# A GRU, attention and AUGRU recommender on one core: attention MLP as three matmuls on shared rows, blockwise softmax, two lagged halves

## The chip, the cores and the metric

The kernel runs on one core of a Trainium2 chip. The core has a matmul engine (TensorE, PE in the profile), a vector engine (VectorE, DVE), an engine for activation functions (ScalarE, ACT), a general one (GpSimd, POOL) and SyncE (SP), which here issues every DMA. Each engine works through its own queue in order; semaphores tie them together. SBUF holds tiles of 128 partitions, matmul results land in PSUM (8 banks, each 128 x 512 in f32), everything larger lies in DRAM. The metric is the device time of one execution in microseconds.

## The reference

A batch of B = 1024 users, T = 100 steps, all widths 128, all in f32. What is computed:

```python
hist_sum = (item_hist * mask[:, :, None]).sum(1) / length[:, None]
# GRU over the 100 steps, all states kept
r = sigmoid(x @ Wir + h @ Whr + b);  z = sigmoid(x @ Wiz + h @ Whz + b)
n = tanh(x @ Win + bin + r * (h @ Whn + bhn))
h = (1 - z) * n + z * h                       # keys[t] = h
# attention: MLP of 512 -> 80 -> 40 -> 1, ReLU after each layer
feat  = concat([keys, q, keys - q, q * keys]) # q: the item's embedding
score = where(mask == 1, mlp(feat), -inf)
pooled = einsum('bt,btd->bd', softmax(score, axis=1), keys)
att = pooled.T[:T]                            # row t weighs step t of the AUGRU
# AUGRU over keys
r = sigmoid([h, k] @ Wr + br);  u = att[t] * sigmoid([h, k] @ Wu + bu)
h = (1 - u) * h + u * tanh([h * r, k] @ Wh + bh)
# state at each user's length, then an MLP of 640 -> 200 -> 80 -> 1 with sigmoids
out = mlp(concat([user, item, hist_sum, item * hist_sum, h_last]))
```

The AUGRU needs the pooled keys, these need the softmax over all 100 scores of a user, and a score needs the GRU's state of its step. Users don't depend on each other.

## The kernel before

Features lie on the partitions and the batch on the free dimension. A PSUM bank holds 512 columns, so the batch is worked in two halves (`HB = 512`, `NH = 2`). One f32 product, `nc.tensor.matmul` of a 128 x 128 weight with 128 x 512 data, appears in the profile as two MATMUL instructions, each with its weight load (PEld). The code is a tile program: it states operations on named tiles, and a scheduler sorts them at compile time into one fixed order for each engine, by their place in the program and by when it reckons them ready, and adds the semaphores. An operation that stands late in the program can so come early in its queue. A pool with `bufs=n` gives n buffers in turn to tiles of one tag; a DMA into a buffer waits until its last reader is done.

The work stands in four stages, one after the other.

1. GRU, attention scores and history sum (loop at L172). For each step t it loads x (512 KB, both halves) and the mask row spread over the partitions. For each half, `gru` (L114) makes six products: the gate r from x and h (L118, with `wih` and `whh`), the two halves of n kept apart, and z. ACT makes r (L129) and z (L134), DVE forms the argument of tanh from PSUM (L136, L139), ACT takes tanh (L141), and three DVE operations (L143 to L145) make the new state `hn`. GpSimd multiplies x by the mask and adds it to `hist` (L183, L184). For each half, `score` (L147) makes `kq` = state times item on DVE (L150), two products for layer 0 (L152, L153: 80 result rows), adds the part of the item alone and takes ReLU (L155, L156), one product of 80 rows for layer 1 (L158), ReLU (L160), and one product of 40 rows for layer 2 (L163). That last one uses a sliding window of a zero matrix with one column, so that the score of step t lands on partition t of a PSUM tile that is kept for the whole stage. The state goes to DRAM (L188), but for the last `RES` = 16 steps, which stay in SBUF.
2. Softmax and pooled keys. The scores are transposed so that users are on partitions, masked, exponentiated, transposed back and written to DRAM. For each of 100 steps the weights' row is loaded spread over the partitions (L256), the keys too (L259, 84 steps), DVE multiplies them (L262), and PE adds them up in PSUM with the identity as weight (L264, 200 products). The pooled rows times one over the sum (L250, L277), zero from a user's length on (L278), go to DRAM.
3. AUGRU (loop at L318). For each step the row of weights `at` and the keys are loaded; for each half `augru` (L295) makes three gates of two products each (L297 to L310), with ACT for sigmoid and tanh (L300, L306, L312), GpSimd for u times at (L307) and DVE for the rest (L301, L313 to L315).
4. Prediction MLP (L339 to L372), 13 products for each half.

Of the kernel before, what the change touches and what calls it, by code (L numbers as in the profile page):

```python
# [17 lines left out]
P = 128  # L18
# [4 lines left out]
NG = B // P  # L23
A0, A1 = 80, 40
M0, M1 = 200, 80
MC = 100
RES = 16
# [3 lines left out]
def kernel(ctx: ExitStack, tc: tile.TileContext, a: dict, out: bass.AP):  # L31
    """Features lie on the partitions and the batch on the free dim throughout.

    1: GRU over the steps, with the attention MLP's scores and the masked history sum.
    2: masked softmax over the steps and the pooled keys.
    3: AUGRU over the steps.
    4: the prediction MLP.
    The keys of the last RES steps stay in SBUF; the others go through DRAM.
    """
# [3 lines left out]
    resp = ctx.enter_context(tc.tile_pool(name="resp", bufs=1))  # L43

    keys_d = dram.tile([T - RES, P, B], F32, name="keys_d")
    mask_d = dram.tile([T, B], F32, name="mask_d")
    e_d = dram.tile([T, B], F32, name="e_d")
    att_d = dram.tile([T, B], F32, name="att_d")
    res = resp.tile([P, RES, B], F32, name="res")
# [7 lines left out]
    mask_ti = load("mask_ti", [T, B], dt=I32)  # L57
# [3 lines left out]
    bhh = load("bhh", [P, 3])  # L61
    item = load("item", [P, B])
    w0 = load("w0", [P, 4, A0])
    b0 = load("b0", [A0, 1])
    w1 = load("w1", [A0, A1])
    b1 = load("b1", [A1, 1])
    b2 = load("b2", [T, 1], a["b2"].partition_broadcast(T))
    w2 = const.tile([A1, 2 * T - 1], F32, name="w2")
    nc.vector.memset(w2, 0.0)
    nc.sync.dma_start(out=w2[:, T - 1 : T], in_=a["w2"])  # L70

    mask_tf = const.tile([T, B], F32, name="mask_tf")
# [5 lines left out]
    ones = const.tile([T, P], F32, name="ones")  # L78
    nc.vector.memset(ones, 1.0)
# [7 lines left out]
    wk = const.tile([P, A0], F32, name="wk")  # L87
    nc.vector.tensor_add(wk, w0[:, 0, :], w0[:, 2, :])
    wq = const.tile([P, A0], F32, name="wq")
    nc.vector.tensor_sub(wq, w0[:, 1, :], w0[:, 2, :])  # L90
# [3 lines left out]
    h0 = const.tile([P, B], F32, name="h0")  # L94
    nc.vector.memset(h0, 0.0)
    q0 = const.tile([A0, B], F32, name="q0")
    s_t = const.tile([T, B], F32, name="s_t")

# [1 line left out]
    with tc.tile_pool(name="xp", bufs=3) as xp, tc.tile_pool(  # L100
        name="hp", bufs=3
    ) as hp, tc.tile_pool(name="wp", bufs=2) as wp, tc.tile_pool(
        name="ps_s", bufs=1, space=PSUM
    ) as ps_s, tc.tile_pool(name="ps_g", bufs=4, space=PSUM) as ps_g, tc.tile_pool(
        name="ps_a", bufs=2, space=PSUM
    ) as ps_a:
        for i in range(NH):
            pq = ps_a.tile([A0, HB], F32, tag="a", name="pq")
            nc.tensor.matmul(pq, lhsT=wq, rhs=item[:, ts(i, HB)], start=True, stop=True)
            nc.scalar.activation(q0[:, ts(i, HB)], pq, AF.Identity, bias=b0)  # L110

        sc = [ps_s.tile([T, HB], F32, tag=f"sc{i}", name=f"sc{i}") for i in range(NH)]

        def gru(x, h, hn, cols):  # L114
            def gate(g, parts):
                ps = ps_g.tile([P, HB], F32, tag="g", name=f"ps{g}")
                for n, (w, v) in enumerate(parts):
                    nc.tensor.matmul(  # L118
                        ps,
                        lhsT=w[:, g, :],  # L120
                        rhs=v[:, cols],
                        start=(n == 0),
                        stop=(n == len(parts) - 1),
                    )
                return ps

            pr = gate(0, ((wih, x), (whh, h)))
            r = wp.tile([P, HB], F32, name="r")
            nc.scalar.activation(r, pr, AF.Sigmoid, bias=brz[:, 0:1])  # L129
            ph = gate(2, ((whh, h),))  # L130
            pi = gate(2, ((wih, x),))
            pz = gate(1, ((wih, x), (whh, h)))
# [3 lines left out]
            nc.vector.scalar_tensor_tensor(  # L136
                out=u, in0=ph, scalar=bhh[:, 2:3], in1=r, op0=ALU.add, op1=ALU.mult
            )
# [4 lines left out]
            nc.vector.tensor_sub(d, h[:, cols], n)  # L143
            nc.vector.tensor_mul(d, z, d)  # L144
            nc.vector.tensor_add(hn[:, cols], n, d)  # L145

        def score(t, k, i):  # L147
            cols = ts(i, HB)
            kq = wp.tile([P, HB], F32, name="kq")
            nc.vector.tensor_mul(kq, k[:, cols], item[:, cols])  # L150
            p0 = ps_a.tile([A0, HB], F32, tag="a", name="p0")
            nc.tensor.matmul(p0, lhsT=wk, rhs=k[:, cols], start=True, stop=False)  # L152
            nc.tensor.matmul(p0, lhsT=w0[:, 3, :], rhs=kq, start=False, stop=True)  # L153
            f0 = wp.tile([A0, HB], F32, name="f0")
            nc.vector.tensor_add(f0, p0, q0[:, cols])  # L155
            nc.scalar.activation(f0, f0, AF.Relu)  # L156
            p1 = ps_a.tile([A1, HB], F32, tag="a", name="p1")
            nc.tensor.matmul(p1, lhsT=w1, rhs=f0, start=True, stop=True)  # L158
            f1 = wp.tile([A1, HB], F32, name="f1")
            nc.scalar.activation(f1, p1, AF.Relu, bias=b1)  # L160
            # Only column t of this window of w2 is not zero: the scores of step t
            # come onto partition t.
            nc.tensor.matmul(  # L163
                sc[i],
                lhsT=w2[:, T - 1 - t : 2 * T - 1 - t],
                rhs=f1,
                start=(t == 0),
                stop=(t == T - 1),
            )

        h = h0
        for t in range(T):  # L172
            x = xp.tile([P, B], F32, name="x")
            nc.sync.dma_start(out=x, in_=a["hist_x"][t])
            m = xp.tile([P, B], F32, name="m")
            nc.sync.dma_start(out=m, in_=mask_d[t].partition_broadcast(P))
            if t < T - RES:
                hn = hp.tile([P, B], F32, name="hn")
            else:
                hn = res[:, t - (T - RES), :]  # L180
            for i in range(NH):
                gru(x, h, hn, ts(i, HB))
            nc.gpsimd.tensor_mul(m, x, m)  # L183
            nc.gpsimd.tensor_add(hist, hist, m)  # L184
            for i in range(NH):
                score(t, hn, i)
            if t < T - RES:
                nc.sync.dma_start(out=keys_d[t], in_=hn)  # L188
            h = hn

        for i in range(NH):
            nc.scalar.activation(s_t[:, ts(i, HB)], sc[i], AF.Relu, bias=b2)

# [1 line left out]
    wr = load("wr", [P, 2, P])  # L195
    wu = load("wu", [P, 2, P])
    wh = load("wh", [P, 2, P])
    br = load("br", [P, 1])
    bu = load("bu", [P, 1])
    bh = load("bh", [P, 1])  # L200
    user = load("user", [P, B])
    m0 = load("m0", [P, 5, M0])
    c0 = load("c0", [MC, M0 // MC])
    m1 = load("m1", [MC, M0 // MC, M1])
    c1 = load("c1", [M1, 1])
    m2 = load("m2", [M1, 1])
    c2 = load("c2", [1, 1])
    len_i = load("len_i", [P, B], a["len_i"].partition_broadcast(P), dt=I32)
    length = const.tile([P, B], F32, name="length")
    nc.vector.tensor_copy(length, len_i)  # L210

# [1 line left out]
    with tc.tile_pool(name="sp", bufs=1) as sp, tc.tile_pool(  # L213
        name="kp", bufs=4
    ) as kp, tc.tile_pool(name="ps_t", bufs=2, space=PSUM) as ps_t, tc.tile_pool(
        name="ps_p", bufs=1, space=PSUM
    ) as ps_p:
        mask_i = sp.tile([P, NG, T], I32, name="mask_i")
        nc.sync.dma_start(out=mask_i, in_=a["mask"].rearrange("(g p) t -> p g t", p=P))
        on = sp.tile([P, NG, T], F32, name="on")  # L220
        nc.vector.tensor_scalar(on, mask_i, 1.0, None, ALU.is_equal)

        # Scores are not negative, so 0 in the masked places leaves the maximum right.
        e = sp.tile([P, NG, T], F32, name="e")
        for g in range(0, NG, 4):
            pt = ps_t.tile([P, 4, P], F32, tag="t", name="pt")
            for j in range(4):
                nc.tensor.transpose(pt[:, j, :T], s_t[:, ts(g + j, P)], ident[:T, :T])
            nc.vector.tensor_mul(e[:, g : g + 4, :], pt[:, :, :T], on[:, g : g + 4, :])
        top = sp.tile([P, NG], F32, name="top")  # L230
        nc.vector.tensor_reduce(top, e, AX.X, ALU.max)
        nc.vector.tensor_sub(e, e, top.unsqueeze(2).to_broadcast([P, NG, T]))
        nc.scalar.activation(e, e, AF.Exp)
        nc.vector.tensor_mul(e, e, on)

        e_t = sp.tile([T, B], F32, name="e_t")
# [203 lines left out]
```

## Time and profile before

| what | value |
|---|---|
| time, median of 3 runs | 3267.64 us (3263.62 to 3268.73) |
| span of the profiled execution, first to last instruction | 3262.5 us |
| DMA traffic | 348.46 MB, mean 107 GB/s |
| loads of keys in stages 2 and 3 | 168 of 512 KB, 6.0 us to landing |
| loads of x, of the mask row | 100 each of 512 KB, 3.7 us to landing |
| granted clock of TensorE, mean | 0.990 |

The profile shows one execution. For it only the span is known; the runs' times also hold what lies around it. A row of instruction groups reads: line, engine, operation, output <- inputs, shapes, count, then busy time, mean duration in ns, the idle time of the engine just before them and what ended it. In the chain of waits each piece is the work that the next piece was waiting for. The granted clock is the share of TensorE's full clock that the throttle let through. TensorE's busy time is modelled for pipelined matmuls; their spacing in the chain is the safer price.

### The profile page before, as it was taken

How to read it: one execution, taken by the hardware profiler on the slowest of the kernel's cores; microseconds unless marked ns; L12 is line 12 of the kernel's file. 1: busy time of each engine (PE TensorE's matmuls, PEld its weight loads, DVE VectorE, ACT ScalarE, POOL GpSimd, SP SyncE). 2: the span in 40 equal slices, each digit the busy share in tenths (PEclk: the TensorE clock that was granted, in tenths of full speed). 3: DMA queues.
4: the chain of work that ended last, by engine and by line, in shares of the span. 5: the costliest groups of instructions: out<-in, count | busy, mean ns of one | idle time of the engine just before them, and what ended most of it. 6: DMA issues, size and time to landing. Idle time of an engine off the chain costs nothing.

```text
span 3262.5 us, 22072 instructions
## 1 busy us (share of the span) xinstructions
PE 3128.4 (96%) x6876; PEld 1163.6 (36%) x6876; DVE 1659.5 (51%) x2325; ACT 1093.2 (34%) x1617; POOL 765.2 (23%) x408
## 2 busy tenths in 40 slices
PE   7999999999999999999999977769999999999998
PEld 2333333333333333333333322224444444444443
DVE  5555554554555555555545544435555555555554
ACT  2333333333333333333333310003434343444433
POOL 3223223223222222232232100002222222222221
PEclk9999999999999999999999979999999999999999
DMA  4222222222222222222211049983333333333110
GB/s 158 84 79 89 84 84 84 84 85 87 81 90 84 78 90 84 79 89 84 75 54 58 20 138 378 397 324 103 99 102 99 101 103 103 103 103 103 65 52 13
DMA packets 98464, 348.46 MB, mean 107 GB/s; under 512 B 13109, under 2 KB 13977, under 8 KB 98346
## 3 DMA queue, kind: packets, MB, share of 16 engines
q1 hardware_dynamic: 98346, 347.05, 31.1%
q8 instruction: 54, 0.88, 0.1%
q14 instruction: 64, 0.52, 0.1%
HBM read 301.73 MB, written 45.27 MB: 106 GB/s over the span
## 4 chain that ended last, share of the span: by engine, by line
PE 80%; DVE 8%; DMA 5%; ACT 4%; issue 1%; SPq 0%; ACTq 0%; DVEq 0%; POOLq 0%; POOL 0%
PE ps L118 27%; PE sc L163 6%; PE p L158 6%; PE pr L297 5%; PE pu L303 5%; PE pr L298 5%; PE pu L304 5%; PE ph L310 5%; PE ph L309 5%; DMA k<-keys_d 4%; PE p L152 3%; PE p L153 3%; DVE d L144 2%; ACT z L134 2%; ACT f L156 2%; DVE hn L145 2%
## 5 line engine op out<-in xcount | busy, mean ns | idle before, releaser
L118 PE MATMUL ps<-x,wih 128*128 128x512 f32 x1200 | 617.6, 610 | 1.0 <-DMA x<-in_hist_x 1.0
L183 POOL TENSOR_TENSOR m<-x,m 128x1024 f32<-128x1024 f32 x100 | 275.3, 2753 | 1322.9 <-DMA x<-in_hist_x 1307.1
L307 POOL TENSOR_TENSOR u<-u,at 128x512 f32<-128x512 f32 x200 | 252.7, 1264 | 1131.6 <-ACT u L306 1131.6
L118 PE MATMUL ps<-hn,whh 128*128 128x512 f32 x1008 | 501.0, 592 | 0.0
L313 DVE TENSOR_TENSOR d<-d,hn 128x512 f32<-128x512 f32 x198 | 137.1, 692 | 459.4 <-ACT d L312 459.4
L155 DVE TENSOR_TENSOR f<-p,q 80x512 f32<-80x512 f32 x200 | 136.6, 683 | 434.7 <-PE p L153 434.7
L118 PEld LDWEIGHTS ps<-x,wih 128*128 128x128 f32 x1200 | 211.9, 189 | 358.2 <-issue 307.0
L156 ACT ACTIVATE f<-f 80x512 f32<-80x512 f32 x200 | 126.0, 630 | 536.0 <-DVE f L155 536.0
L118 PEld LDWEIGHTS ps<-hn,whh 128*128 128x128 f32 x1008 | 191.6, 190 | 245.4 <-issue 225.3
L264 PE MATMUL pool<-eb,ident 128*128 128x512 f32 x400 | 197.8, 623 | 63.1 <-DVE eb L262 63.0
L141 ACT ACTIVATE n<-u,bih 128x512 f32<-128x512 f32 x200 | 144.4, 722 | 306.9 <-DVE u L139 306.9
L158 PE MATMUL p<-f,w 80*40 80x512 f32 x400 | 212.2, 612 | 28.0 <-ACT f L156 28.0
L184 POOL TENSOR_TENSOR hist<-hist,m 128x1024 f32<-128x1024 f32 x100 | 235.5, 2355 | 7.8
L163 PE MATMUL sc<-f,w 40*100 40x512 f32 x400 | 221.7, 634 | 0.8 <-ACT f L160 0.8
L144 DVE TENSOR_TENSOR d<-z,d 128x512 f32<-128x512 f32 x200 | 142.4, 712 | 155.8 <-ACT z L134 154.9
L136 DVE SCALAR_TENSOR_TENSOR u<-ps,bhh,r 128x512 f32<-128x512 f32 x200 | 150.2, 751 | 126.6 <-PE ps L118 123.7
L153 PE MATMUL p<-kq,w 128*80 128x512 f32 x400 | 212.5, 613 | 1.7 <-DVE kq L150 1.7
L129 ACT ACTIVATE r<-ps,brz 128x512 f32<-128x512 f32 x200 | 137.2, 686 | 226.2 <-PE ps L118 225.7
L312 ACT ACTIVATE d<-ph,bh 128x512 f32<-128x512 f32 x200 | 137.4, 687 | 206.8 <-PE ph L310 206.8
L306 ACT ACTIVATE u<-pu,bu 128x512 f32<-128x512 f32 x200 | 137.4, 687 | 205.5 <-PE pu L304 205.5
L300 ACT ACTIVATE r<-pr,br 128x512 f32<-128x512 f32 x200 | 137.4, 687 | 204.1 <-PE pr L298 204.1
L310 PE MATMUL ph<-r,wh 128*128 128x512 f32 x400 | 204.3, 592 | 0.0
(113 smaller groups left out, 3546.4 us busy)
## 6 DMA issues: line engine op xcount, KB each, us to landing
k<-keys_d SPq DMA_DIRECT2D x168, 512.0 KB, 6.0
x<-in_hist_x SPq DMA_DIRECT2D x100, 512.0 KB, 3.7
m<-mask_d SPq DMA_DIRECT2D x100, 512.0 KB, 3.7
eb<-e_d SPq DMA_DIRECT2D x100, 512.0 KB, 5.5
at<-att_d SPq DMA_DIRECT2D x100, 512.0 KB, 4.5
keys_d<-hn SPq DMA_DIRECT2D x84, 512.0 KB, 2.6
item<-in_item SPq DMA_DIRECT2D x1, 512.0 KB
user<-in_user SPq DMA_DIRECT2D x1, 512.0 KB, 4.9
```

The costliest lines, as they stand in the source:

```text
L118: nc.tensor.matmul(ps, lhsT=w[:, g, :], rhs=v[:, cols], start=(n == 0), stop=(n == len(parts) - 1),)
L144: nc.vector.tensor_mul(d, z, d)
L153: nc.tensor.matmul(p0, lhsT=w0[:, 3, :], rhs=kq, start=False, stop=True)
L156: nc.scalar.activation(f0, f0, AF.Relu)
L158: nc.tensor.matmul(p1, lhsT=w1, rhs=f0, start=True, stop=True)
L163: nc.tensor.matmul(sc[i], lhsT=w2[:, T - 1 - t : 2 * T - 1 - t], rhs=f1, start=(t == 0), stop=(t == T - 1),)
L183: nc.gpsimd.tensor_mul(m, x, m)
L184: nc.gpsimd.tensor_add(hist, hist, m)
L264: nc.tensor.matmul(pool[i], lhsT=ident, rhs=eb[:, ts(i, HB)], start=(n == 0), stop=(n == T - 1),)
L297: nc.tensor.matmul(pr, lhsT=wr[:, 1, :], rhs=k[:, cols], start=True, stop=False)
L307: nc.gpsimd.tensor_mul(u, u, at[:, cols])
L310: nc.tensor.matmul(ph, lhsT=wh[:, 0, :], rhs=r, start=False, stop=True)
```

## The change

The whole computation is kept; its order and its layout change.

- *Shared rows.* The attention MLP's hidden rows lie side by side on 128 partitions: rows 0 to 39 hold layer 1, rows 40 to 95 and 97 to 120 layer 0, and row 96 the score (`F1`, `F0` and `SC` in the diff). The step's `attend` adds three products into one PSUM tile: `wk` on the state, `wkq` on state times item, `w12` on the tile `mv` of the attend before, which holds layer 0 of step t - 1 and layer 1 of step t - 2 (w12 holds the weights of layers 1 and 2). One DVE addition and one ReLU serve the three layers. A score so comes out two steps late, as row 96 of `mv`, and a DMA copies it to its row of a block tile `s_b`.
- *Blocks.* Scores are collected in three blocks that end at steps 48, 92 and 100 (`ENDS`). When a block is complete, `softmax` transposes it, takes the running maximum, exponentiates, adds to the running sum and writes the weights and the factor for what was pooled so far to DRAM.
- *Pooling on VectorE.* `pool` loads a row of weights and a step's keys (256 KB each) and does a multiplication and an addition into `pooled` in SBUF; one key a step, or two when more are left than steps; all that is left after the last step.
- *Two streams.* Each half is an object of its own. Half 1 runs `LAG` = 5 ticks behind half 0, and a half starts its AUGRU `GAP` = 4 ticks after its last GRU tick. All pools are open for the whole kernel; GRU and AUGRU share six PSUM buffers, attention and softmax have two.
- Loads are for 512 columns; all keys go through DRAM (`RES` is gone); step 0 leaves out the products with the zero state; a half's part of the history features and its prediction MLP are emitted in its own stream.

The diff, cut to its core:

```diff
-RES = 16
+F1 = slice(0, A1)
+F0 = (slice(A1, 96), slice(97, 121))
+W0 = (slice(0, 96 - A1), slice(96 - A1, A0))
+SC = 96
+ENDS = (48, 92, T)
+LAG = 5
+GAP = 4
...
+    for f, s in zip(F0, W0):
+        nc.vector.tensor_add(wk[:, f], w0[:, 0, s], w0[:, 2, s])
+        nc.vector.tensor_copy(wkq[:, f], w0[:, 3, s])
+        nc.vector.tensor_sub(wq[:, f], w0[:, 1, s], w0[:, 2, s])
+        nc.sync.dma_start(out=w12[f, F1], in_=a["w1"][s, :])
...
+    nc.sync.dma_start(out=w12[F1, SC : SC + 1], in_=a["w2"])
...
+    xp = ctx.enter_context(tc.tile_pool(name="xp", bufs=5))
+    hp = ctx.enter_context(tc.tile_pool(name="hp", bufs=8))
+    wp = ctx.enter_context(tc.tile_pool(name="wp", bufs=3))
+    sp = ctx.enter_context(tc.tile_pool(name="sp", bufs=2))
+    kp = ctx.enter_context(tc.tile_pool(name="kp", bufs=4))
+    ps = ctx.enter_context(tc.tile_pool(name="ps", bufs=6, space=PSUM))
+    pa = ctx.enter_context(tc.tile_pool(name="pa", bufs=2, space=PSUM))
...
+        def gru(self, t):
+            cols = self.cols
+            x = xp.tile([P, HB], F32, name="x")
+            nc.sync.dma_start(out=x, in_=a["hist_x"][t][:, cols])
+            m = xp.tile([P, HB], F32, name="m")
+            nc.sync.dma_start(out=m, in_=mask_d[t, cols].partition_broadcast(P))
...
+            nc.gpsimd.tensor_mul(m, x, m)
+            nc.gpsimd.tensor_add(hist[:, cols], hist[:, cols], m)
+            nc.sync.dma_start(out=keys_d[t][:, cols], in_=hn)
+            self.h = hn
...
+        def attend(self, t):
+            parts = []
+            if t < T:
+                kq = wp.tile([P, HB], F32, name="kq")
+                nc.vector.tensor_mul(kq, self.h, item[:, self.cols])
+                parts += [(wk, self.h), (wkq, kq)]
+            if self.mv is not None:
+                parts += [(w12, self.mv)]
+            p = pa.tile([P, HB], F32, tag="a", name="pm")
+            for n, (w, v) in enumerate(parts):
+                nc.tensor.matmul(
+                    p, lhsT=w, rhs=v, start=(n == 0), stop=(n == len(parts) - 1)
+                )
+            f = wp.tile([P, HB], F32, name="f")
+            nc.vector.tensor_add(f, p, q0[:, self.cols])
+            mv = wp.tile([P, HB], F32, name="mv", bufs=4)
+            nc.scalar.activation(mv, f, AF.Relu)
+            self.mv = mv
+            s = t - 2
...
+            nc.sync.dma_start(out=self.s_b[s - a0 : s - a0 + 1, :], in_=mv[SC : SC + 1, :])
+            if s == ENDS[self.block] - 1:
+                self.softmax()
...
+        def softmax(self):
...
+            nc.vector.tensor_mul(e[:, :, :n], pt[:, :, :n], on)
+            top = sp.tile([P, GH], F32, name="top", bufs=5)
+            nc.vector.tensor_reduce(top, e[:, :, :n], AX.X, ALU.max)
+            if j:
+                nc.vector.tensor_max(top, top, self.top)
+                nc.vector.tensor_sub(e[:, :, n], self.top, top)
...
+            nc.scalar.activation(e[:, :, :rows], e[:, :, :rows], AF.Exp)
+            nc.vector.tensor_mul(e[:, :, :n], e[:, :, :n], on)
+            den = sp.tile([P, GH], F32, name="den", bufs=5)
+            nc.vector.tensor_reduce(den, e[:, :, :n], AX.X, ALU.add)
...
+            nc.sync.dma_start(out=e_d[j][:rows, self.cols], in_=e_t[:rows, :])
+            if j:
+                self.todo.append((j, n, None))
+            self.todo += [(j, t - a0, t) for t in range(a0, a1)]
+            if last:
+                self.todo.append((j, n + 1, None))
...
+        def pool(self, count):
+            for _ in range(min(count, len(self.todo))):
+                j, row, t = self.todo.pop(0)
+                eb = kp.tile([P, HB], F32, name="eb")
+                nc.sync.dma_start(out=eb, in_=e_d[j][row, self.cols].partition_broadcast(P))
+                acc = pooled[:, self.cols]
+                if t is None:
+                    nc.vector.tensor_mul(acc, acc, eb)
+                    continue
+                k = kp.tile([P, HB], F32, name="k")
+                nc.sync.dma_start(out=k, in_=keys_d[t][:, self.cols])
+                if t == 0:
+                    nc.vector.tensor_mul(acc, k, eb)
+                else:
+                    nc.vector.tensor_mul(eb, k, eb)
+                    nc.vector.tensor_add(acc, acc, eb)
...
+    for tick in range(2 * T + GAP + LAG):
+        if tick == 2:
+            load_later()
+        now = [(half, tick - LAG * half.i) for half in halves]
+        for half, s in now:
+            if 0 <= s < T:
+                half.gru(s)
+            elif T + GAP <= s < 2 * T + GAP:
+                half.augru(s - T - GAP)
+        for half, s in now:
+            if 0 <= s < T:
+                half.attend(s)
+                half.pool(2 if len(half.todo) > T - s else 1)
+            elif s == T:
+                half.attend(T)
+                half.attend(T + 1)
+                half.pool(len(half.todo))
+                half.weights()
+            elif s == T + GAP + 10:
+                half.features()
+            elif s == 2 * T + GAP - 1:
+                half.predict()
```

What stands at "..." is either as before on half the columns (the gates of `gru` and of the AUGRU, the prediction MLP), the loading of later weights (`load_later`, emitted at tick 2), or `weights`, which masks a half's pooled rows by the users' lengths and writes them to DRAM.

More of the change, by code (lines that the diff above doesn't have):

```diff
@@ L23 @@
 NG = B // P
+GH = HB // P
 A0, A1 = 80, 40
@@ L92 @@
     hist = const.tile([P, B], F32, name="hist")
     nc.gpsimd.memset(hist, 0.0)
-    h0 = const.tile([P, B], F32, name="h0")
+    h0 = const.tile([P, HB], F32, name="h0")
     nc.vector.memset(h0, 0.0)
[L96 to L114, printed above, removed]
+    q0 = const.tile([P, B], F32, name="q0")
@@ L142, in gru @@
             d = wp.tile([P, HB], F32, name="d")
-            nc.vector.tensor_sub(d, h[:, cols], n)
+            nc.vector.tensor_sub(d, h if t else h0, n)
             nc.vector.tensor_mul(d, z, d)
[L145 to L168, printed above, removed]
-            )
@@ L171 @@
[L171 to L178, printed above, removed]
-            else:
[L180 to L207, printed above, removed]
@@ L335 @@
-    with tc.tile_pool(name="fp", bufs=1) as fp, tc.tile_pool(
-        name="ps4", bufs=2, space=PSUM
-    ) as ps4:
-        rlen = fp.tile([P, B], F32, name="rlen")
-        nc.vector.reciprocal(rlen, length)
-        nc.vector.tensor_mul(hist, hist, rlen)
-        cross = fp.tile([P, B], F32, name="cross")
-        nc.vector.tensor_mul(cross, item, hist)
-        comb = (user, item, hist, cross, h)
-        y = fp.tile([1, B], F32, name="y")
-        for i in range(NH):
-            cols = ts(i, HB)
-            f0 = fp.tile([MC, M0 // MC, HB], F32, name="g0", bufs=2)
+            nc.vector.tensor_add(hn, n, d)
```

335 lines of the change are left out of this document (186 added, 149 removed).

## The prediction

> **What bounds the kernel now.** I read the page first: the busy shares and the shares of the chain that ended last.
>
> ```profile
> span 3262.5 us, 22072 instructions
> PE 3128.4 (96%) x6876; PEld 1163.6 (36%) x6876; DVE 1659.5 (51%) x2325; ACT 1093.2 (34%) x1617; POOL 765.2 (23%) x408
> PE 80%; DVE 8%; DMA 5%; ACT 4%; issue 1%; SPq 0%; ACTq 0%; DVEq 0%; POOLq 0%; POOL 0%
> ```
>
> TensorE (PE) is busy 96% of the span and holds 80% of the chain. An average hides stages, so next the busy time by window, cut at the stage borders (us; then PE, PEld, DVE, ACT, POOL busy with their instructions, the granted clock, DMA share, GB/s):
>
> ```profile
> 0.00:13.50 13.50, 3.61 (x5) 0.89 (x5) 2.59 (x8) 2.91 (x4) 1.67 (x8) 1.00 0.74 216
> 13.50:1908.50 1895.00, 1862.02 (x4000) 623.97 (x4000) 975.59 (x1402) 668.50 (x1002) 510.75 (x200) 0.99 0.24 80
> 1908.50:2194.80 286.30, 203.87 (x422) 73.52 (x421) 137.20 (x112) 2.84 (x3) 0.00 (x0) 0.95 0.90 346
> 2194.80:3220.90 1026.10, 1026.10 (x2385) 454.26 (x2386) 530.84 (x793) 410.06 (x597) 250.21 (x198) 1.00 0.29 93
> 3220.90:3262.50 41.60, 32.79 (x68) 10.91 (x66) 13.34 (x11) 8.90 (x13) 2.52 (x2) 0.91 0.00 0
> ```
>
> These are start, GRU, softmax with pooling, AUGRU and end. GRU and AUGRU are bound by PE; the middle stage, 286.3 us, is bound by its loads (DMA share 0.90). The length of one GRU step (both halves) shows in the issue times of the same load, one step apart, in the timeline of the SP queue:
>
> ```profile
> 804.88 0.33 SPq L174 DMA_DIRECT2D x<-in_hist_x  x1
> 823.59 0.33 SPq L174 DMA_DIRECT2D x<-in_hist_x  x1
> ```
>
> So 18.71 us a step. The chain of waits inside it, and two pieces of the AUGRU's chain, give the price of a product (one matmul call, two MATMUL instructions):
>
> ```profile
> 800.36 5.36 PE ps L118 x12
> ...
> 809.32 1.05 PE p L158 x2
> 810.37 1.02 PE p L152 x2
> 811.38 1.03 PE sc L163 x2
> ...
> 813.43 1.72 PE ps L118 x4
> ...
> 2600.28 0.86 PE pr L298 x2
> ...
> 2610.58 0.86 PE pr L298 x2
> ```
>
> Among full 128-row weights a product takes 0.86 us (1.72 / 2); around the products with 80 and 40 rows it takes 1.02 to 1.05. An AUGRU step, both halves, lasts 10.30 us, which is its 12 products.
>
> **The change part by part.**
>
> *Products.* A GRU step has 20 (12 gates, 4 for layer 0, 2 for layer 1, 2 for layer 2) and keeps 18: layers 1 and 2 become one product with w12. All are 128 rows wide now, so the surcharge goes too: 18 x 0.86 = 15.5 us in place of 18.71. Pooling's 200 products on the identity go. The AUGRU keeps 12.
>
> *VectorE (DVE).* Per half it has 7 operations a GRU step today; pooling adds 2 for each key. Their spacing is read from the DVE timeline:
>
> ```profile
> 806.52 0.69 DVE L144 TENSOR_TENSOR d<-z,d 128x512 f32<-128x512 f32 x1 [0.20 <-ACT z L134]
> 807.25 0.69 DVE L145 TENSOR_TENSOR hn<-n,d 128x512 f32<-128x512 f32 x1
> 807.86 0.68 DVE L155 TENSOR_TENSOR f<-p,q 80x512 f32<-80x512 f32 x1
> 808.46 0.68 DVE L150 TENSOR_TENSOR kq<-hn,item 128x512 f32<-128x512 f32 x1
> ```
>
> An operation that needs the one before starts 0.73 us after it, an independent one 0.60; I take 0.66. Both halves: 14 operations, 9.2 us, while nothing is pooled (steps 0 to 48 of a half); 18, 11.9 us, with one key a step (49 to 92); 22, 14.5 us, with two (93 to 99). That is below 15.5, but DVE isn't alone. At the start POOL and DVE run together:
>
> ```profile
> 18.09 2.35 POOL L183 TENSOR_TENSOR m<-x,m 128x1024 f32<-128x1024 f32 x1 [15.85 <-DMA m<-mask_d]
> 20.51 2.67 POOL L184 TENSOR_TENSOR hist<-hist,m 128x1024 f32<-128x1024 f32 x1
> 18.76 2.22 DVE L143 TENSOR_TENSOR d<-h,n 128x512 f32<-128x512 f32 x1 [0.79 <-ACT n L141]
> 21.09 2.65 DVE L144 TENSOR_TENSOR d<-z,d 128x512 f32<-128x512 f32 x1
> ```
>
> DVE's 0.69 us operation lasts until 20.98, that is 0.54 us after POOL's ended at 20.44; the next one ends 0.56 us after POOL's next. They take turns. In the steady steps POOL works in DVE's gap. With DVE fuller that gap shrinks, so it has a price: POOL's four half-width operations a step, each as long as this one:
>
> ```profile
> L307 POOL TENSOR_TENSOR u<-u,at 128x512 f32<-128x512 f32 x200 | 252.7, 1264 | 1131.6 <-ACT u L306 1131.6
> L136 DVE SCALAR_TENSOR_TENSOR u<-ps,bhh,r 128x512 f32<-128x512 f32 x200 | 150.2, 751 | 126.6 <-PE ps L118 123.7
> ```
>
> 4 x 1.26 = 5.0 us at most, nothing at least (all in gaps). I take 3.5, since DVE reads PSUM in 6 operations a step (as in L136) and those kept 0.75 us beside POOL. Then DVE needs 12.7, 15.4 and 18.0 us against PE's 15.5. Two engines that full don't mesh perfectly, so I set steps of **15.6, 16.4 and 17.5 us** (the last because the halves pool twice in different steps, 5 apart). The Trainium skill, SBUF — State Buffer, "SBUF: two separate sides", says that the pair of ports which GpSimd shares with VectorE is an exclusive lock for a whole instruction against VectorE operations with two SBUF inputs; the start agrees (2.22 and 2.65 us). By it each of the four can cost its full length, and the second rival would be the forecast.
>
> *Transfers.* RES goes, all keys pass through DRAM, tiles are halves: 10 of 256 KB a step, 2.6 MB in 16 us, 164 GB/s. The middle stage moved 398:
>
> ```profile
> 2000.00:2100.00 100.00, 76.14 (x155) 26.02 (x155) 46.56 (x38) 0.00 (x0) 0.00 (x0) 1.00 1.01 398
> 1908.00:1920.00 12.00, 5.01 (x19) 3.35 (x19) 5.51 (x7) 2.84 (x3) 0.00 (x0) 0.50 0.47 177
> ```
>
> So they hide under PE; on SP 12 issues x 0.33 = 4 us a step do too. Where such a load is late, the pool's multiply waits on DVE, and behind it stand the other half's gate operations, for which PE waits; that is priced in the second rival. Early loads and new weight tiles I cost at nothing: they run beside the first steps.
>
> *Blocks.* A key enters the pool when its block's softmax is done. Blocks 0 and 1 finish at steps 49 and 93, so at the last step about 45 keys are left in each half (48 - 44 = 4, plus a rescale and 44, less 7 x 2, plus 10 rows of the last block). This drain is the serial part: 45 x 2 DVE operations, 1.36 us a key with the mean of the rows above = 61 us; by bytes 512 KB / 398 GB/s = 1.32 us, the same. Around it:
>
> ```profile
> 1909.39 1.58 PE pt L228 x8
> 1910.97 6.11 issue
> 1917.08 1.92 PE pe L240 x8
> ...
> 2184.55 3.61 DMA att_d<-att
> 2189.20 5.58 DMA at<-att_d
> ```
>
> A softmax takes 9.6 us from the first transpose to the last (I use 10), the weights' way through DRAM 10.5 (2184.55 to 2194.8). The 16 transposes above take 3.5 us at half clock; the four earlier softmaxes have 8 each, some 1 us, and wait for table loads: between 0 and 10 each, I take 2.5, so 10.
>
> *Lag.* Half 1 runs 5 steps behind: half 0 is alone at first, 5 x 9 us (9 products are 7.7, its chain of 6.1, worked out below, partly uncovered). An AUGRU step alone:
>
> ```profile
> 2600.12 1.02 PE L298 MATMUL pr<-hn,wr 128*128 128x512 f32 x2
> 2601.18 0.69 ACT L300 ACTIVATE r<-pr,br 128x512 f32<-128x512 f32 x1 [1.03 <-PE pr L298]
> ```
>
> From a product's start to its reader 1.06, twice; two activations 1.4, four DVE operations of 0.73, 2.9: 6.4; with launches 7, against 5.2 of PE. In half 1's drain, with DVE contested, 9. (A lone GRU chain has one such product, two activations and five DVE operations: 6.1.)
>
> **Sum**: start 13.5; lone 45; 44 x 15.6 = 686; 44 x 16.4 = 722; 7 x 17.5 = 122; softmaxes 10: half 0 ends its GRU at 1598. From there 10 + 61 + 10.5: its AUGRU starts at 1680. Half 1's last five steps need 5 x 11 x 0.66 = 36 us of DVE beside the drain, so it ends at 1598 + 107 = 1705. Its own drain, 10 + 61 + 10.5 + 10 for half 0's interleaved operations: 1797. Meanwhile half 0 does (1797 - 1680) / 9 = 13 steps. The remaining 87 together, 87 x 10.3 = 896: 2693. Half 1's last 13 alone, 91: 2784. End:
>
> ```profile
> 3228.10 6.55 DVE rlen L339
> ...
> 3236.38 7.84 PE p L351 x12
> ```
>
> The reciprocal moves under the AUGRU, half 0's MLP too; half 1's 13 products and latencies: 18. Span 2802. The shown runs' median, 3267.64, stands 5.1 above the profiled span, which is that execution's only time I have; so **2805** for the time.
>
> **Rivals.**
>
> *PE alone decides.* POOL finds gaps; all 95 common steps last 15.5 (1472, 58 less), softmaxes cost nothing (10 less), half 1's steps fit under a drain of 85 (22 less): 2710. For it: GRU and AUGRU are PE-bound now and the order of instructions is planned. Against: DVE's free time per step falls from 9 us to 3.
>
> *DVE decides.* Turns with POOL cost their full 5 us and an in-order queue adds waits for late loads: steps of 16.5, 18.5, 20.5: 726 + 814 + 144 = 1684, 154 more: 2960. The same if pooling falls behind and more keys are left for the drain. For it: the start's rows.
>
> *Half clock while one half runs alone.* The window 1908 to 1920 was granted 0.50 after idle PE. If lone steps trigger it, an AUGRU step costs 10.3: 13 x 3.3 = 43, and 5 x 5 at the start: 2875. Against: window 2000 to 2100 had PE busy 76% at 1.00. The Trainium skill, TensorE: Matmul & The Clock Gate, "HAM oscillation — how this bites in real kernels", puts the drop at idle gaps over some 3.4 us; the lone AUGRU's gaps I estimate at about 1.5.
>
> *Slower: SP's queue.* The copy of a score row waits for the last ReLU of the step. If the next step's x is queued behind it, PE waits each step for ReLU 0.63, three issues 1.0 and the landing:
>
> ```profile
> x<-in_hist_x SPq DMA_DIRECT2D x100, 512.0 KB, 3.7
> ```
>
> 5.3 x 95 = 504: 3310. It decides once a step loses over (3267 - 2805) / 95 = 4.9 us. Against: five x buffers, two and a half steps ahead.
>
> **Chances.** Forecast 0.50 (own range 2750 to 2860), PE alone 0.18, DVE 0.20, clock 0.08, SP 0.04. The range 2680 to 2980 takes in all but SP's case and the tails of DVE's (drains of over 100 us). Differences below 0.2% can't be told from no change here. Only SP's case is slower: faster 0.95, same 0.01, slower 0.04.
>
> **What would show it.** Right: gate products 0.86 apart with no 1.02 pieces; x issues 15.5 to 16 us apart before step 49, over 16 after; DVE operations of over 1 us beside POOL's; two stretches of 80 to 110 us in mid-run with PE half empty; 10.3 us an AUGRU step; PE instructions near 6080. Wrong: steps over 18 us, PE waiting for x, lone steps at clock 0.5, or drains of half or twice 61 us.

## The result, and the profile after

| | time, median | ratio to before (95% interval) |
|---|---|---|
| before | 3265.63 us | |
| after | 2923.95 us (2921.34 to 2925.43) | 0.895 (0.8938 to 0.8963) |
| forecast | 2805 us (2680 to 2980) | |

The change saves 342 us. The direction and the stated range held. The saving was forecast 119 us too large, and the forecast's own narrower range, 2750 to 2860 us, was missed: the time lies nearer to its second rival, 2960 us. The page of the changed kernel, with the rows that answer to those shown first in the prediction:

```profile
span 2923.5 us, 22860 instructions
PE 2686.5 (92%) x6080; PEld 1153.6 (39%) x6080; DVE 1898.7 (65%) x2674; ACT 970.0 (33%) x1431; POOL 846.8 (29%) x615
PE 58%; DVE 24%; issue 7%; DMA 6%; ACT 4%; SPq 1%; POOL 1%; DVEq 0%; ACTq 0%; POOLq 0%
```

PE runs the 6080 instructions that were counted, but its share of the chain that ended last fell from 80% to 58%, and DVE's rose from 8% to 24%. The span cut at the events that the trace shows (columns as in the prediction: window, PE, PEld, DVE, ACT, POOL busy with instructions, clock, DMA share, GB/s):

```profile
0.00:94.50 94.50, 64.81 (x131) 26.26 (x132) 51.08 (x66) 22.70 (x34) 37.28 (x37) 0.93 0.55 171
94.50:817.00 722.50, 689.60 (x1586) 296.87 (x1585) 462.48 (x618) 236.64 (x354) 250.29 (x178) 1.00 0.29 97
817.00:1203.00 386.00, 336.77 (x737) 141.01 (x736) 344.81 (x467) 109.67 (x165) 123.68 (x78) 0.96 0.63 204
1203.00:1590.00 387.00, 367.75 (x844) 158.04 (x843) 248.85 (x330) 124.64 (x187) 134.31 (x94) 1.00 0.30 96
1590.00:1705.00 115.00, 99.26 (x224) 41.56 (x222) 104.96 (x150) 33.12 (x50) 35.58 (x24) 0.96 0.65 210
1705.00:1910.00 205.00, 122.09 (x231) 48.14 (x231) 171.41 (x280) 41.47 (x60) 22.53 (x13) 0.76 0.78 246
1910.00:2873.00 963.00, 963.00 (x2245) 425.92 (x2244) 500.44 (x748) 386.90 (x563) 236.75 (x187) 1.00 0.32 102
2873.00:2923.50 50.50, 43.19 (x92) 15.77 (x90) 14.73 (x22) 14.81 (x22) 6.34 (x5) 0.93 0.05 15
```

From the top: the start; GRU steps without pooling; GRU steps beside the pooling of the first block, DVE busy 344.8 of 386 us (nothing is pooled from 839 to 919 us); steps without pooling again; the second block's first keys; the drains of both halves, PE busy 122 of 205 us and its granted clock 0.76; the AUGRU of both halves, PE busy all the time; half 1's last steps and the end. The pooling doesn't run at one key a step for half the GRU, as the program writes it. In the order that the scheduler made, 89 of the first block's 96 keys go by between 826 and 1201 us, 83 of them after 919; the other 7 come with the second block.

The surprise is in the second row: there is no pooling in it, and still its steps are longer than 18 products. One such step in the timeline (start, length, engine):

```profile
314.01 0.69 DVE L218 TENSOR_TENSOR hn<-n,d 128x512 f32<-128x512 f32 x1
...
324.62 1.49 POOL L219 TENSOR_TENSOR m<-x,m 128x512 f32<-128x512 f32 x1 [6.72 <-DMA x<-in_hist_x]
...
325.02 1.64 DVE L230 TENSOR_TENSOR kq<-hn,item 128x512 f32<-128x512 f32 x1
...
326.19 1.60 POOL L220 TENSOR_TENSOR hist<-hist,m 128x512 f32<-128x512 f32 x1
326.58 0.74 DVE L207 SCALAR_TENSOR_TENSOR u<-ps,bhh,r 128x512 f32<-128x512 f32 x1
...
330.49 0.69 DVE L218 TENSOR_TENSOR hn<-n,d 128x512 f32<-128x512 f32 x1
...
331.24 1.12 PE L236 MATMUL pm<-hn,wk 128*128 128x512 f32 x2 [0.76 <-DVE hn L218]
```

From 314.01 to 330.49 the same half's state comes 16.48 us apart, as in nearly all of these steps. GpSimd's multiply starts when its x lands, at 324.62. DVE's `kq` of one half starts 0.40 us later, reads two SBUF tiles and takes 1.64 us in place of 0.69: it ends 0.55 us after GpSimd's end at 326.11. Behind it in DVE's queue stands `u` of the *other* half. That half's state is late by as much, and PE idles 0.76 us until it comes. Beside pooling the same happens several times a step:

```profile
825.54 0.69 DVE L218 TENSOR_TENSOR hn<-n,d 128x512 f32<-128x512 f32 x1
...
1036.08 1.75 DVE L318 TENSOR_TENSOR pooled<-pooled,eb 128x512 f32<-128x512 f32 x1
1037.75 1.75 DVE L217 TENSOR_TENSOR d<-z,d 128x512 f32<-128x512 f32 x1
...
1193.16 1.16 DVE L218 TENSOR_TENSOR hn<-n,d 128x512 f32<-128x512 f32 x1
```

From the first to the last row 38 states are made, 19 steps of both halves: 367.6 / 19 = 19.35 us each. A few of these steps have no key to pool; from 917 us, with 83 keys in 14.5 steps, the mean is 19.7. Operations of 0.69 us take 1.75 while GpSimd works.

### The profile page after: what moved, and what is told of

It reads as the page before. It is cut to its first block, busy times and chain, and to the rows that moved or that the text cites. A ratio compares the mean times of both kernels' runs of the same rounds, so it can differ in the third digit from the quotient of the medians.

```text
span 2923.5 us, 22860 instructions
## 1 busy us (share of the span) xinstructions
PE 2686.5 (92%) x6080; PEld 1153.6 (39%) x6080; DVE 1898.7 (65%) x2674; ACT 970.0 (33%) x1431; POOL 846.8 (29%) x615
## 4 chain that ended last, share of the span: by engine, by line
PE 58%; DVE 24%; issue 7%; DMA 6%; ACT 4%; SPq 1%; POOL 1%; DVEq 0%; ACTq 0%; POOLq 0%
PE ps L186 14%; PE pm L236 9%; PE pr L349 6%; PE ph L349 6%; PE pu L349 6%; PE pu L347 6%; PE ph L347 6%; PE pr L347 6%; DVE d L217 4%; DVE hn L218 4%; DMA k<-keys_d 3%; DVE d L216 3%; DVE eb L317 3%; DVE u L207 3%; DVE u L212 3%
## 5 line engine op out<-in xcount | busy, mean ns | idle before, releaser
L219 POOL TENSOR_TENSOR m<-x,m 128x512 f32<-128x512 f32 x200 | 289.9, 1449 | 1109.7 <-DMA x<-in_hist_x 1084.8
L236 PE MATMUL pm<-hn,wk 128*128 128x512 f32 x400 | 224.4, 644 | 138.2 <-DVE hn L218 138.2
L220 POOL TENSOR_TENSOR hist<-hist,m 128x512 f32<-128x512 f32 x200 | 292.3, 1461 | 15.7
L240 DVE TENSOR_TENSOR f<-pm,q 128x512 f32<-128x512 f32 x204 | 140.0, 686 | 135.6 <-PE pm L236 135.4
L236 PE MATMUL pm<-kq,wkq 128*128 128x512 f32 x400 | 218.2, 629 | 10.4 <-DVE kq L230 10.1
L347 PE MATMUL pr<-k,wr 128*128 128x512 f32 x396 | 204.6, 598 | 23.5 <-DMA k<-keys_d 23.5
L216 DVE TENSOR_TENSOR d<-hn,n 128x512 f32<-128x512 f32 x198 | 139.4, 704 | 127.1 <-ACT n L214 127.1
L349 PE MATMUL pr<-hn,wr 128*128 128x512 f32 x396 | 206.1, 602 | 16.5 <-DVE hn L368 15.3
L230 DVE TENSOR_TENSOR kq<-hn,item 128x512 f32<-128x512 f32 x200 | 212.4, 1062 | 5.2
L236 PE MATMUL pm<-mv,w 128*128 128x512 f32 x404 | 211.5, 605 | 2.2 <-ACT mv L242 2.2
```

Source lines behind the costliest of these rows:

```text
L216: nc.vector.tensor_sub(d, h if t else h0, n)
L220: nc.gpsimd.tensor_add(hist[:, cols], hist[:, cols], m)
L230: nc.vector.tensor_mul(kq, self.h, item[:, self.cols])
L236: nc.tensor.matmul(p, lhsT=w, rhs=v, start=(n == 0), stop=(n == len(parts) - 1))
L240: nc.vector.tensor_add(f, p, q0[:, self.cols])
L347: nc.tensor.matmul(p, lhsT=w[:, 1, :], rhs=k, start=True, stop=v is None)
```

## The experiments

Two theories stood against each other for the 16.48 us. **Port theory**: VectorE and GpSimd take turns at SBUF, and the turn that falls on `kq` costs PE its wait. **Order theory**: PE's planned order holds that wait whatever GpSimd does, or VectorE has too much work. A second question was what bounds the drains, and a third what the parts of the change are worth.

### GpSimd without work in the GRU

```diff
-            nc.gpsimd.tensor_mul(m, x, m)
-            nc.gpsimd.tensor_add(hist[:, cols], hist[:, cols], m)
```

> The changed kernel without GpSimd's two operations a GRU step and half (the history sum stays zero; its loads stay). Port theory: in the changed kernel a GRU step without pooling lasts 16.48 us, because GpSimd's multiply holds VectorE's kq (1.17 us in the mean in place of 0.69), behind which the other half's u waits, and PE then waits 0.76 us for hn; without GpSimd kq takes 0.69 us, the step 15.5 to 15.8 us, and the whole 2780 to 2850 us. Rival, order theory: PE's planned order has that wait for hn anyway; the step stays at 16.2 to 16.5 us, the whole at 2900 to 2925.

Measured: 2755.05 us, 169 less, more than the port theory's own range. Its group of `kq` (count, then busy time and mean ns) and its busy time between 300 and 600 us:

```profile
L228 DVE TENSOR_TENSOR kq<-hn,item 128x512 f32<-128x512 f32 x39 | 27.0, 692 | 1.3
```

```profile
300.00:600.00 300.00, 299.82 (x696) 130.40 (x695) 186.37 (x272) 105.55 (x155) 0.00 (x0) 1.00 0.21 69
```

The same two views of the changed kernel:

```profile
L230 DVE TENSOR_TENSOR kq<-hn,item 128x512 f32<-128x512 f32 x36 | 40.3, 1119 | 1.2
```

```profile
300.00:600.00 300.00, 287.25 (x660) 123.65 (x659) 190.16 (x254) 97.95 (x147) 102.72 (x74) 1.00 0.29 96
```

`kq` is back from 1.12 to 0.69 us in the mean, and PE idles 0.2 us in 300 in place of 12.8. A step has 36 MATMULs, so 696 are 19.3 steps of 15.5 us, the forecast price of 18 products. Steps beside the first block's pooling, counted in the same way, fell from 19.35 to 15.8 us. That is where the range was too narrow: the turns cost 0.9 us in a free step, but over 3 us in a pooled one. Half 0 ends its GRU at 1541 us here and at 1709 in the changed kernel, so 168 of the 169 us are lost before that point.

Leaving work out can't tell the turns from VectorE's load or from the x buffers that GpSimd holds. The next two keep all the work.

### The history on VectorE

```diff
-            nc.gpsimd.tensor_mul(m, x, m)
-            nc.gpsimd.tensor_add(hist[:, cols], hist[:, cols], m)
+            nc.vector.tensor_mul(m, x, m)
+            nc.vector.tensor_add(hist[:, cols], hist[:, cols], m)
```

> The changed kernel with the history's multiply and add on VectorE in place of GpSimd, so that GpSimd has no work in a GRU step. Port theory: four more VectorE operations a step (some 2.6 us) cost less than the turns with GpSimd: kq 0.69 us, steps without pooling 15.5 to 15.7 us as when the history was left out, pooled steps 17 to 18.5 us, the whole 2780 to 2850 us. Rival, load theory: it is VectorE's sheer work that lengthens the steps; free steps 16.3 us or more, the whole 2920 us or more.

Measured: 2809.76 us, ratio 0.8606 (0.8575 to 0.8638). The same window:

```profile
300.00:600.00 300.00, 297.24 (x684) 127.17 (x683) 221.92 (x342) 98.56 (x152) 0.00 (x0) 1.00 0.31 101
```

VectorE does *more* (221.9 us in 300, against 190.2 in the changed kernel) and the steps are shorter: 684 MATMULs, 15.8 us a step, a little over the port theory's 15.5 to 15.7. The load theory falls. Pooled steps took 16.2 us, less than expected; here the same 89 keys were spread over 445 us in place of 375, so each step had fewer.

### The same GpSimd work at another moment

```diff
-    xp = ctx.enter_context(tc.tile_pool(name="xp", bufs=5))
+    xp = ctx.enter_context(tc.tile_pool(name="xp", bufs=6))
...
-            nc.gpsimd.tensor_mul(m, x, m)
-            nc.gpsimd.tensor_add(hist[:, cols], hist[:, cols], m)
+            self.x, self.m = x, m
...
-                nc.vector.tensor_mul(kq, self.h, item[:, self.cols])
+                self.kq = nc.vector.tensor_mul(kq, self.h, item[:, self.cols])
...
+        def history(self, after):
+            cols = self.cols
+            i1 = nc.gpsimd.tensor_mul(self.m, self.x, self.m)
+            tc.add_manual_dep(
+                i1.ins, after.ins.name, mybir.DependencyInfo(
+                    mybir.DependencyClass.Sync, mybir.DependencyReason.DATA)
+            )
+            nc.gpsimd.tensor_add(hist[:, cols], hist[:, cols], self.m)
...
             if 0 <= s < T:
                 half.attend(s)
+                last = half.kq
+        for half, s in now:
+            if 0 <= s < T:
+                half.history(last)
                 half.pool(2 if len(half.todo) > T - s else 1)
```

> The changed kernel with GpSimd's four operations of a step kept, but the first of each half made to wait for half 1's kq (both attends are emitted ahead of both pools for it; six x buffers in place of five), so that they fall into the 7 us in which VectorE reads PSUM or idles. Port theory: nothing meets them in a step without pooling, kq 0.69 us, 15.5 to 15.7 us a step; pooled steps have no such stretch and stay near 19 us; some 60 free steps x 0.9 us: 2855 to 2890 us. Rival, order theory: the step stays 16.4 us and the time within 15 us of 2924.

Measured: 2841.26 us, ratio 0.8703 (0.867 to 0.8736), 14 us better than the range. The window from 300 to 600 us,

```profile
300.00:600.00 300.00, 299.81 (x697) 130.26 (x696) 186.45 (x272) 105.51 (x155) 94.06 (x76) 1.00 0.30 101
```

and its groups of `kq` and of GpSimd's multiply:

```profile
L229 DVE TENSOR_TENSOR kq<-hn,item 128x512 f32<-128x512 f32 x39 | 27.0, 692 | 1.3
L256 POOL TENSOR_TENSOR m<-x,m 128x512 f32<-128x512 f32 x38 | 47.4, 1268 | 201.4 <-DVE kq L229 201.4
```

GpSimd has the same operations, only later, and the step is at 15.5 us. This is the cleanest of the three: the same instructions, moved by a wait into the stretch from `kq` to the next gate's tanh, where VectorE reads PSUM or idles. Two more things changed with the wait, the sixth x buffer and the place of the pooling in the program; what each does alone wasn't run. The first two experiments, with five buffers and the old order, reached 15.5 and 15.8 us too. Pooled steps keep 18.8 us; VectorE's gap is filled there. So the port theory's account is shown: `kq` is held while GpSimd works, and PE pays for it.

### The attention MLP alone

The kernel before, with its `score` replaced by the `attend` of the change (weights wk, wkq and w12 laid out as there; the score row copied by DMA to its row of `s_t`; six PSUM buffers for the gates), everything else as it was.

```diff
-            p0 = ps_a.tile([A0, HB], F32, tag="a", name="p0")
...
+            parts = []
+            if t < T:
+                kq = wp.tile([P, HB], F32, name="kq")
+                nc.vector.tensor_mul(kq, k[:, cols], item[:, cols])
+                parts += [(wk, k[:, cols]), (wkq, kq)]
+            if mvs[i] is not None:
+                parts += [(w12, mvs[i])]
...
+            nc.vector.tensor_add(f, p, q0[:, cols])
+            mv = wp.tile([P, HB], F32, name="mv", bufs=4)
+            nc.scalar.activation(mv, f, AF.Relu)
+            mvs[i] = mv
+            if t >= 2:
+                nc.sync.dma_start(out=s_t[t - 2 : t - 1, cols], in_=mv[SC : SC + 1, :])
```

> The kernel before with the attention MLP as three products on shared rows and nothing else of the change: softmax, pooling, stages and full-width tiles as before. If the products carry the gain, its GRU step falls from 18.71 us to 16.3 to 17.0 and the time to 3040 to 3110 us, so that more than half of the change's 342 us is here. Rival: the step is bound by the chain of one step and GpSimd's 2.4 us operations hold VectorE longer than the half-width ones; step over 17.5 us, time over 3150.

Measured: 2953.26 us, ratio 0.9047 (0.9015 to 0.908), better than either theory. A window within its GRU stage:

```profile
500.00:1000.00 500.00, 499.86 (x1158) 217.00 (x1157) 308.59 (x449) 173.52 (x258) 158.17 (x66) 1.00 0.29 102
```

1158 MATMULs in 500 us are 15.5 us a step, with GpSimd's full-width operations in it: in this order they fall into VectorE's gap, as they did in the kernel before, and `kq` keeps its 0.69 us:

```profile
L161 DVE TENSOR_TENSOR kq<-hn,item 128x512 f32<-128x512 f32 x64 | 44.3, 692 | 2.2
```

So the three products bring 312 us (3265.8 - 2953.3) of the change's 342. The two more PSUM buffers for the gates weren't tried alone; they can have brought little, since PE idled only 33 us in the whole GRU stage of the kernel before. All the rest of the change, which removes a stage of 286 us, brings 30 more: its GRU lasts until 1709 us where this one's ends near 1590, and the drains come in the stage's place.

### Without the lag

```diff
-LAG = 5
+LAG = 0
```

> The changed kernel with LAG = 0 in place of 5: both halves end their GRU together and drain together. Theory that the lag buys little: the drains of both halves already run as one stretch of about 200 us with PE half empty; without the lag it has about 70 us less PE work beside it, which must be done elsewhere, and the lone steps at the start (some 20 us) and the end (some 12) go: 2920 to 2970 us. Rival, the lag hides one drain: 2990 us or more.

Measured: 2949.58 us, 26 more, in the first theory's range. The busy tenths of its PE over 40 slices of the span show the drains with nothing beside them, in slices 25 and 26:

```profile
PE   7999999999988888999999982099999999999999
```

The lag is worth about 1% here.

### What bounds a drain

Three edits of `pool`: the keys' load replaced by the item's columns; the addition left out; both.

```diff
-                k = kp.tile([P, HB], F32, name="k")
-                nc.sync.dma_start(out=k, in_=keys_d[t][:, self.cols])
+                k = item[:, self.cols]
```

```diff
-                    nc.vector.tensor_mul(eb, k, eb)
-                    nc.vector.tensor_add(acc, acc, eb)
+                    nc.vector.tensor_mul(acc, k, eb)
```

> The changed kernel in which pooling multiplies the weights with the item's columns in place of the step's keys, so that the 200 key loads of pooling go and its operations stay (pooled values are not the reference's). If the drain is bound by VectorE, the stretch with PE half empty keeps its 200 us and the time falls by under 15 us. If transfers bind it (DMA share 0.69 to 0.84 there), it shrinks towards 150 us and the time falls by 40 us or more.

> The changed kernel in which pooling multiplies only and adds nothing (a key overwrites the pooled tile), so that one of two VectorE operations a key goes and all loads stay. If VectorE binds the drain, it shrinks by some 60 us, and with shorter pooled steps the time falls by 70 to 110 us. If transfers bind it, the drain keeps its length and only the pooled steps gain: under 50 us.

> Both halvings at once: pooling multiplies only, and takes the item's columns in place of the step's keys, so that a key needs one VectorE operation and 256 KB. If VectorE and the transfers bound the drain at nearly the same length (1.33 us a key by operations, 1.32 us by bytes), each hid behind the other before; now the stretch with PE half empty falls from 200 us to 110 to 140, pooled steps shorten too, and the time is 2800 to 2865 us. Rival, the planned order alone sets its length: the stretch stays over 180 us, the time at 2890 us or more.

Measured: 2925.33, 2946.35 and 2861.52 us, a single run each. The window from 1800 to 1850 of the changed kernel, then of the first two, and from 1850 to 1900 of the third:

```profile
1800.00:1850.00 50.00, 35.42 (x77) 13.83 (x75) 46.25 (x78) 12.49 (x18) 10.26 (x4) 0.86 0.80 250
```

```profile
1800.00:1850.00 50.00, 39.03 (x85) 15.72 (x83) 46.51 (x75) 14.03 (x21) 4.94 (x3) 0.91 0.51 157
```

```profile
1800.00:1850.00 50.00, 42.04 (x88) 17.57 (x89) 36.88 (x48) 11.59 (x18) 7.07 (x6) 0.92 0.78 231
```

```profile
1850.00:1900.00 50.00, 49.52 (x115) 21.64 (x115) 28.13 (x41) 21.10 (x31) 13.17 (x10) 1.00 0.31 95
```

With half the bytes VectorE is still busy 46.5 of 50 us, and the whole gains nothing. With half the operations VectorE falls to 36.9, transfers stay at a share of 0.78, and the time rises by 22 us, which neither theory had. With both the AUGRU runs at full speed by 1850, and the time lies within the range that was expected.

The total hides where each edit acts. In VectorE's timelines a drain can be cut out by two rows, the last GRU state of half 0 and the AUGRU weights of half 1, which follow its last key. For the changed kernel, half the bytes, half the operations, and both:

```profile
1708.95 1.75 DVE L218 TENSOR_TENSOR hn<-n,d 128x512 f32<-128x512 f32 x1
1898.84 0.75 DVE L324 SCALAR_TENSOR_TENSOR att<-length,step,pooled 100x512 f32<-100x512 f32 x1
```

```profile
1724.27 0.68 DVE L218 TENSOR_TENSOR hn<-n,d 128x512 f32<-128x512 f32 x1
1893.07 1.75 DVE L323 SCALAR_TENSOR_TENSOR att<-length,step,pooled 100x512 f32<-100x512 f32 x1
```

```profile
1736.21 0.69 DVE L218 TENSOR_TENSOR hn<-n,d 128x512 f32<-128x512 f32 x1
1909.91 0.75 DVE L323 SCALAR_TENSOR_TENSOR att<-length,step,pooled 100x512 f32<-100x512 f32 x1
```

```profile
1707.76 0.68 DVE L218 TENSOR_TENSOR hn<-n,d 128x512 f32<-128x512 f32 x1
1837.39 0.75 DVE L322 SCALAR_TENSOR_TENSOR att<-length,step,pooled 100x512 f32<-100x512 f32 x1
```

The drains last 190, 169, 174 and 130 us. One halving alone takes 21 or 16 us off, both together 60, more than their sum. So the two bounds of the prediction, 1.36 us a key by operations and 1.32 by bytes, were both real, and each largely hid the gain of removing the other. The two single halvings lost their gain before the drain: half 0's GRU ended 15 and 27 us later. With half the operations the record shows where. In the steps beside the first block (911 to 1215 us) VectorE now waits for loads of keys, with the gate operations behind it in its queue; the changed kernel's row stands first:

```profile
L317 DVE TENSOR_TENSOR eb<-k,eb 128x512 f32<-128x512 f32 x82 | 69.5, 864 | 7.6 <-DMA k<-keys_d 7.6
L317 DVE TENSOR_TENSOR pooled<-k,eb 128x512 f32<-128x512 f32 x82 | 75.1, 925 | 39.0 <-DMA k<-keys_d 38.7
```

A step there took 21.8 us in place of 19.7. What lengthened the GRU steps with half the bytes the runs don't follow.

### Five blocks in place of three, and a version that gains

```diff
-ENDS = (48, 92, T)
+ENDS = (48, 72, 84, 92, T)
```

> The changed kernel with five blocks, ENDS = 48, 72, 84, 92, 100 in place of 48, 92, 100: some 35 keys fewer for each half remain for the drain. Theory: pooling beside GRU steps costs about 0.45 us a key (95 keys lengthened the steps by 40 us in the changed kernel), in the drain 1.45 us; 70 keys x 1.0 us less 10 us for four more softmaxes: 2855 to 2885 us. Rival: these late steps are full already, and what the drain loses the steps gain: 2910 to 2940 us.

Measured: 2930.66 us, the rival. Late GRU steps (1278 to 1695 us) took some 20 us each, and what the drain lost they gained: half 0's GRU ended at 1776 us, 67 later. Then with the history on VectorE as above:

> History on VectorE and five blocks (48, 72, 84, 92, 100) together, the whole computation kept. Without GpSimd a pooled key lengthened the GRU steps by only some 15 us for 95 keys, 0.15 us each. Port theory: what made the five blocks useless alone were the turns with GpSimd in the late steps; now some 70 keys leave the drain at 1.3 us each, less 20 us for softmaxes and fuller steps: 2725 to 2770 us. Rival: late steps fill up on VectorE as before: 2795 to 2825 us.

> The same with LAG = 0. With a short drain there is little to hide behind the other half, and the lone steps at the start and end (some 30 us) go: 2700 to 2750 us, below the version with the lag. Rival, the lag still hides a drain: 15 us or more above the version with the lag.

Measured: 2751.82 us, ratio 0.8418 (0.8403 to 0.8433), and without the lag 2760.15 us, 0.8445 (0.8433 to 0.8458). The same edit that gained nothing beside GpSimd gains 58 us without it (2809.8 to 2751.8): pooled steps stay at 16.3 us. The lag's worth fell from 26 us to 8, between the two theories: neither range held it. The version with both edits beats the kernel before by 16% and the changed one by 172 us.

## Why the prediction was right, and where it was wrong

**Right, in the products, the AUGRU and the drains.** The products: 18 at 0.86 us make 15.5 us, and the surcharge of the 80- and 40-row weights is gone; the MLP alone and the gated version run at that price. The AUGRU: 10.3 us a step. The drains: forecast 199 us from half 0's last GRU step until both AUGRUs run, measured 1910 - 1709 = 201. Their two bounds were equal, as the rows had said. From there to the end the forecast had 1005 us, measured 1014; that sum is closer than its terms, since 67 us more of joint AUGRU steps (963 for 896) stand against 58 less of half 1's lone end and the final MLP (50.5 for 109). SP's queue didn't hold up x: PE waited 0.6 us for it in all, by this row of the page, though 23.5 us for loads of keys in the drains.

```profile
L186 PE MATMUL ps<-x,wih 128*128 128x512 f32 x1200 | 586.6, 596 | 0.6 <-DMA x<-in_hist_x 0.6
```

Two slips in the sum are small: the weights' way through DRAM is 10.25 us by its own two times, not 10.5, and 2802 and 5.1 make 2807, not 2805.

**Wrong in one size.** The step that failed is the price of VectorE's turns with GpSimd. The prediction gave POOL 3.5 of 5.0 us a step, *added* it to VectorE's total and compared the total with PE's: 12.7 against 15.5, so a free step of 15.6. The chain doesn't work by totals. One blocked operation stands at the head of an in-order queue, the other half's chain is behind it, and PE's order has nothing else to do at that moment. Measured: 16.48 in free steps (0.9 more than forecast), 19.35 beside pooling (16.4 forecast, though for fewer keys at a time). Half 0's 93.5 steps from 94.5 to 1709 us took 17.27 us in the mean, forecast 16.2: some 99 of the 121 us by which the span missed. The start adds 12 more: the lone steps took some 12 us each where 9 was forecast; why wasn't followed. That the stated range still held is owed to its width, which took in the second rival.

**The second rival** (VectorE decides, 2960 us) named this mechanism and its place, with steps of 16.5 and 18.5 us; the time fell between it and the forecast, 36 us from the rival and 119 from the forecast. Its reason, a full queue, was half the truth: with more work on VectorE and none on GpSimd the kernel was faster by 114 us.

**Wrong in the order.** The pooling was taken from the program's text, one key a step. The scheduler's order was denser, so 44 steps at 16.4 were really 19 at 19.35 and some 25 free ones; what the same keys cost at one a step no run shows. Half 0 did 6 AUGRU steps in half 1's drain, not 13: VectorE was busy 171 of the 205 us there, with the pooling in the same queue, and PE waited for keys. What it lost there was done at full speed later, and half 1's lone end shrank from 13 forecast steps to 5.

**The lone steps' clock** (a rival with 0.08) played no part in half 1's last steps, clock 1.00 from 2873 to 2905 us, and some in the drains, 0.76, where PE idled 83 of 205 us, and at the start, 0.85 from 13 to 60 us.

## What to carry to other kernels

Price a shared resource by *which* instruction it delays, not by its share of the time: look for what stands behind that instruction in the same in-order queue and whether the bound engine then has other work. Before moving work to an engine that shares SBUF with another, look where the other's operations fall; an added wait that moves them into a stretch of PSUM reads, with one more x buffer, was worth 83 us here. And when two bounds are of nearly equal length, remove both in one experiment and measure the stretch itself: with one removed the total said that neither counts.

## What the runs showed of the hardware that was not expected

- GpSimd is slowed by the turns too: its multiply of 128x512 took 1.39 to 1.45 us in the changed kernel and 1.27 when nothing met it (the gated version's row above).
- The VectorE operations with a PSUM input kept their time beside GpSimd: `u` took 0.74 us at 326.58 while GpSimd ran from 326.19 to 327.79. This is what the Trainium skill states in SBUF — State Buffer, "SBUF: two separate sides": the lock is only against VectorE operations with two SBUF inputs or in a mode that uses both ports. On the first the runs agree (`kq` 1.64 us, `u` 0.74); the second no run here shows.
